# Graph attention, 1 core: TensorE's projection units are taken out of order, and a bank's second product follows its reader by a step

## The chip, the cores and the metric

The kernel runs on one core of a Trainium2 chip. Its engines are TensorE (PE in the profile), VectorE (DVE), ScalarE (ACT), GpSimd (POOL) and SyncE (SP), which issues transfers. The metric is the device time of one run in microseconds (us); lower is better.

## What is computed

The input x has 16 batches of 1024 nodes with 512 features, in float32; adj is one sparse 1024 x 1024 matrix of zeros and ones for all batches. Each batch goes through one layer of masked attention with 8 heads, a residual sum and a layer norm:

```python
q, k, v = x @ Wq + bq, x @ Wk + bk, x @ Wv + bv      # 8 heads of 64 features
scores = q @ k.T / sqrt(64), where adj is 0: -1e9
out = softmax(scores) @ v
result = layernorm(x + out @ Wo + bo)
```

## The kernel before

**Work and tiles.** A batch's 1024 nodes are 8 tiles of 128 rows. The rows of K and V are written to DRAM, and GpSimd gathers from there, for each tile of nodes, the rows that its nodes are linked to, one gather ("block") at a time. VectorE multiplies q with the gathered keys (`qk`) and reduces to scores (`s`), ScalarE takes the exponentials and weighs the values (`pv`), TensorE or VectorE adds the weighed values up (`sum`), VectorE normalises (`o`), TensorE transposes (`poT`) and multiplies with Wo (`po`), and VectorE and ScalarE make the residual sum and the layer norm (`y`, `stats`).

**The order of the work.** The program is written out under a manual schedule: the loop at the end of the main function runs over steps n, one for each block, and every engine runs its instructions in the order in which this loop issues them. In each step it issues the attention work of the blocks near n; then it spends a credit, in us of TensorE, on units from one of two lists: `finishing` (the products po of a finished tile) if there are any, otherwise `fronts` (all projections of all batches, in order). Transposes poT and the mean product pm come through a third list, `urgent`. Each unit is a tuple of its cost, a function that issues it, and a test whether it is ready. The loop looks only at the first unit of the list; if that isn't ready, the step ends. `later(k, fn)` puts the issue of fn k steps later. "Ready" is a matter of this writing order, not of time on the chip: an instruction that depends on another is safe in any case, and waits on a semaphore where its input isn't there yet.

**The projections of two tiles.** The function `pair` lists the units for x tiles 2j and 2j+1 of batch b. Keys and values of the two are made with seven half products in place of eight (Strassen's scheme in Winograd's form): on VectorE the sums s1 to s4 of the transposed tiles (`combine`, L783 to L786), and then on TensorE, each a unit of two matmuls into a 128 x 512 bank (L956):

1. bank x: A11·B11, read by ScalarE's copy e (L969)
2. bank p6: s2·T2, read by VectorE's w (L972)
3. q0: four matmuls of the query product pq of the first tile (L799)
4. bank x again: + A12·B21, which goes on top and needs the copy e first; read by ScalarE as the keys of the first tile (L835)
5. bank p7: s3·T3, read by VectorE's g (L975)
6. the transposes pxT of the next two x tiles (L757); ScalarE copies each to `xT` (L761), and a step after the second copy `combine` makes the next pair's s1 to s4
7. bank z: s1·T1, read by VectorE's kv (L984), which sets R["v1"]
8. q1: pq of the second tile (left out for tile 1 from batch 1 on, so in pair 0)
9. bank p4: A22·T4, read by VectorE's kv (L979)
10. bank z again: + s4·B22, which needs the read of L984 first; read by VectorE as the values of the first tile (L988)

After the tenth the second tile of K and V is sent to DRAM by SyncE, VectorE adds the values to `vsum` (L860 to L863), and after the last pair of a batch TensorE takes their mean, pm (L867). The products x, z and p write float32 with the two matmuls of a unit; the banks x and z exist once each, and four more banks ("fill") serve p6, p7, p4, pq, po, pxT, poT and pm in turn.

The unit's test before is `(need is None or need in R) and (b, j) in SX and bool(combined)`: the second product into x is ready as soon as e is in R, so in the very step in which the copy was issued, and that into z as soon as the read was issued. q products have no test.

Of the kernel before, what the change touches and what calls it, by code (L numbers as in the profile page):

```python
# [71 lines left out]
LAST_SHARE = 3.4  # L72
BIAS = 0.22

P = 128
# [103 lines left out]
def kernel(  # L179
# [62 lines left out]
    W = {}  # L242
# [12 lines left out]
    with ExitStack() as main:  # L255
# [6 lines left out]
        def fill_psum(name):  # L262
            return psum.tile([P, HALF], F32, tag="fill", name=name, bufs=4)
# [472 lines left out]

        BOTH = {}
        X, XT, SX, KV, VSUM, NRM, Y, OT, PS = {}, {}, {}, {}, {}, {}, {}, {}, {}
        set_up = {}
# [12 lines left out]
        def transpose_x(b, t):  # L752
            def pe():
# [25 lines left out]

                def combine():  # L780
                    s = [work.tile([P, HD2], F32, tag=f"s{i}", name=f"s{i}_{b}_{t}", bufs=1 + i // 4) for i in (1, 2, 3, 4)]
                    x0, x1 = XT[b, t - 1], XT[b, t]
                    nc.vector.tensor_tensor(s[0], x1[:, 0:HD2], x1[:, HD2:D], op=OP.add)  # L783
                    nc.vector.tensor_tensor(s[2], x0[:, 0:HD2], x1[:, 0:HD2], op=OP.subtract)
                    nc.vector.tensor_tensor(s[1], s[0], x0[:, 0:HD2], op=OP.subtract)
                    nc.vector.tensor_tensor(s[3], x0[:, HD2:D], s[1], op=OP.subtract)  # L786
                    SX[b, t // 2] = s
# [4 lines left out]

        def product(name, lhs, w, out):

            def unit(c):
                if c == 0:
                    PS[name] = fill_psum(name)
                p = PS[name]
                nc.tensor.matmul(p, lhs(c), w[:, c, :], start=(c == 0), stop=(c == NPAIR - 1))  # L799
                if c == NPAIR - 1:  # L800
                    del PS[name]
                    later(1, lambda: out(p))

            return [(PRODUCT, lambda c=c: unit(c), None) for c in range(NPAIR)]

# [10 lines left out]
        def pair(b, j):  # L816
# [62 lines left out]
            def lone_product():  # L879
# [24 lines left out]

                return [(4 * BIAS, pe, None)]

            def lhs(i):
                return lambda c: XT[b, tt[i]][:, ts(c, P)]

            q0, q1 = (  # L910
                product(f"pq_{b}_{tt[i]}", lhs(i), W["q"], lambda p, i=i: out_q(i, p)) if b == 0 or tt[i] != ONE_KEY else []
                for i in range(2)
            )
            if j == 0 and b >= PAIRED_FROM:
                q0 = []
                if merged(b):
                    q0 = product(f"pq_{b}_0", lambda c: BOTH[b // 2][:, 1, c, :], W["q"], lambda p: out_q(0, p))
                    q0 += lone_product()
# [28 lines left out]

            def unit(bank, left, right, first, after, need):
                def pe():
                    if first:  # L950
                        R[bank] = fill_psum(f"p{bank}_{b}_{j}") if bank[0] == "p" else psum.tile(
                            [P, HALF], F32, tag=bank, name=f"{bank}_{b}_{j}", bufs=1
                        )
                    l = left()
                    for c in range(2):
                        nc.tensor.matmul(  # L956
                            R[bank], l[:, ts(c, P)], right[:, c, :], start=(first and c == 0), stop=(c == 1),
                            skip_group_check=True,
                        )
                    later(1, after)  # L960

                return [(2 * PRODUCT, pe, lambda: (need is None or need in R) and (b, j) in SX and bool(combined))]

# [4 lines left out]
            def out_e():  # L968
                nc.scalar.copy(temp("e"), R["x"])  # L969

            def out_w():
# [5 lines left out]
            def out_k1():  # L977
                kv = KV[b, tt[1]]
                nc.vector.tensor_tensor(kv[:, 0:D], R["p4"], R["g"], op=OP.add)  # L979
                send(1)  # L980
                later_last(1, lambda: norm(b, tt[1], kv[:, 0:D]))

            def out_v1():
                nc.vector.tensor_tensor(new_kv(1)[:, D:], R["z"], R["g"], op=OP.add)  # L984
                R["v1"] = True

            def out_v0():
                nc.vector.tensor_tensor(KV[b, tt[0]][:, D:], R["z"], R["w"], op=OP.add)  # L988
                send(0)

            def s(i):
# [5 lines left out]
            units += q0  # L997
            units += unit("x", lambda: a(0, 1), B21, False, lambda: out_k(0, R["x"]), "e")
            units += unit("p7", s(3), T3, True, out_g, None)
# [499 lines left out]
        def paced(share, n):  # L1499
# [3 lines left out]
            return share * load_of(n) * (start[b + 1] - start[b]) / sum(load_of(m) for m in range(start[b], start[b + 1]))  # L1503

        prep = {}
        for t, n in REST_FROM.items():
# [9 lines left out]
        with tc.manual_schedule():  # L1516
# [21 lines left out]
            while n < total or plan or rest or urgent or done or finishing or spilled or lone_tiles or not guarded:  # L1538
# [53 lines left out]
                while credit > 0 or urgent:  # L1592
# [10 lines left out]
                    if not units:  # L1603
# [3 lines left out]
                        break  # L1607
                    cost, fn, ready = units[0]
                    if ready and not ready():
                        if urgent:  # L1610
                            urgent.pop(0)()
                            continue
                        break
                    del units[0]
                    fn()
# [42 lines left out]
```

## Time and profile before

| | us |
|---|---|
| time, median of 3 runs | 1847.21 |
| fastest and slowest run | 1845.62, 1847.80 |
| the profiled execution: span from the first to the last instruction | 1840.4 |
| the profiled execution's own time outside its span | not recorded |
| TensorE busy | 1798.2 |
| VectorE busy | 1693.7 |
| ScalarE busy | 1563.2 |
| GpSimd busy | 1215.3 |
| mean granted TensorE clock | 0.996 |

The profile is of one execution. A row of the timeline gives the start, the duration, the engine, the line, the operation with its output and inputs, the shapes, and how many such instructions follow each other (x4). Matmuls are pipelined, so a row's duration overlaps with the next row; what a product takes is read from start to start. One 128 x 512 float32 product leaves two records of a matmul, so a unit of two is a row "x4". Where an engine idled before a row, the row ends with that idle time and with what it waited for. Line numbers of the profile before are those of the code above; in the changed kernel they stand some lines lower (L956 is L971, L799 is L805, L757 is L759, L761 is L763, L984 is L1005, L867 is L873).

### The profile page before, as it was taken

To read this page: it belongs to the slowest core of one execution; us is meant where nothing else is said; L and a number is where in the kernel's file an instruction comes from. 1 tells how busy PE (TensorE), PEld (TensorE's weight loads), DVE (VectorE), ACT (ScalarE), POOL (GpSimd) and SP (SyncE) were. 2 spreads that over 40 slices of the span, in tenths; PEclk is the share of its full clock that TensorE was granted. 3 is DMA by queue.
4 is the path that set the end of the run, shared out by engine and by line. 5 is a ranking of instruction groups with operands and counts; after the bars stand their busy time and mean duration, and the time that the engine had idled before them with its cause. 6 is when DMAs were issued, how large, how long until landed. Compare 5 with 4: busy or idle time off the path is not lost.

```text
span 1840.4 us, 25352 instructions
## 1 busy us (share of the span) xinstructions
PE 1798.2 (98%) x5140; PEld 876.2 (48%) x5140; DVE 1693.7 (92%) x3473; ACT 1563.2 (85%) x6183; POOL 1215.3 (66%) x1142
## 2 busy tenths in 40 slices
PE   7999999999999999999999999999999999999997
PEld 3444454554444454444444445444544444444443
DVE  6889889999989999999999999999999999997986
ACT  3637869989889898999889988989799999987886
POOL 1367766766565776767757666677666767665786
PEclk9999999999999999999999999999999999999998
DMA  7358787989889899999988998999989999889995
GB/s 287 106 190 253 256 325 237 346 301 327 308 280 314 295 336 319 344 316 308 347 316 310 346 335 276 343 321 322 339 315 325 314 355 326 306 324 325 338 319 191
DMA packets 198791, 558.54 MB, mean 303 GB/s; under 512 B 33450, under 2 KB 33470, under 8 KB 198626
## 3 DMA queue, kind: packets, MB, share of 16 engines
q0 software_dynamic: 112640, 370.50, 59.3%
q1 hardware_dynamic: 82910, 180.52, 26.2%
q10 hardware_dynamic: 3076, 5.82, 0.9%
q14 instruction: 122, 1.00, 0.2%
q8 instruction: 43, 0.70, 0.2%
HBM read 420.30 MB, written 157.45 MB: 314 GB/s over the span
## 4 chain that ended last, share of the span: by engine, by line
PE 69%; DVE 10%; ACT 9%; DMA 4%; issue 3%; POOL 1%; SPq 0%; POOLq 0%; DVEq 0%; ACTq 0%
PE po L799 17%; PE pq L799 15%; PE pp L956 12%; PE z L956 9%; PE x L956 9%; ACT pv L1341 5%; DVE qk L1313 2%; PE poT L1401 2%; PE pxT L757 2%; PE sum L1367 2%; DVE s L1317 2%; PE sum L1366 2%; DVE pv L1357 1%; ACT sq_k L809 1%; DMA kvg<-kv_pair,place_row 1%
## 5 line engine op out<-in xcount | busy, mean ns | idle before, releaser
L1341 ACT ACTIVATE pv<-kvg,pv 128x64 f32<-128x64 f32 x3600 | 907.5, 341 | 0.0
L1292 POOL DMA_INDIRECT kvg<-kv_pair,place_row x462 | 526.7, 1140 | 307.4 <-ACT pv L1341 99.6
L799 PE MATMUL pq<-wq,xT 128*128 128x512 f32 x792 | 367.8, 596 | 0.0
L1317 DVE TENSOR_REDUCE s<-qk 128x8 f32<-128x512 f32 x530 | 360.7, 681 | 6.8
L799 PE MATMUL po<-wo,oT 128*128 128x512 f32 x792 | 359.3, 594 | 0.7 <-ACT oT L1405 0.7
L1313 DVE TENSOR_TENSOR qk<-qt,kvg 128x512 f32<-128x512 f32 x434 | 297.2, 685 | 1.1 <-DMA kvg<-kv_rows,key_row 0.6
L956 PE MATMUL x<-b,xT 128*128 128x512 f32 x504 | 237.3, 593 | 0.5 <-ACT e L969 0.4
L956 PE MATMUL pp<-t,s 128*128 128x512 f32 x504 | 237.0, 593 | 0.0
L1357 DVE TENSOR_TENSOR pv<-pv,pv 128x520 f32<-128x520 f32 x329 | 228.3, 694 | 4.3 <-ACT pv L1341 4.2
L799 PEld LDWEIGHTS po<-wo,oT 128*128 128x128 f32 x792 | 149.1, 191 | 170.0 <-issue 160.2
L799 PEld LDWEIGHTS pq<-wq,xT 128*128 128x128 f32 x792 | 148.4, 192 | 161.9 <-issue 149.9
L1010 POOL DMA_INDIRECT x<-in_x_dram,asked_row x120 | 133.0, 1108 | 77.8 <-issue 21.3
L1148 POOL DMA_INDIRECT out_dram<-y,asked_row x129 | 146.9, 1139 | 39.1 <-issue 21.2
L1328 ACT ACTIVATE pv<-s,absent 128x8 f32<-128x8 f32 x434 | 127.0, 294 | 44.0 <-DVE s L1317 40.8
L809 ACT ACTIVATE sq_k<-kv 128x128 bf16<-128x128 f32 x512 | 150.8, 301 | 6.4 <-DVE kv L979 3.4
L956 PEld LDWEIGHTS pp<-t,s 128*128 128x128 f32 x504 | 94.7, 191 | 108.1 <-issue 99.4
L956 PEld LDWEIGHTS x<-b,xT 128*128 128x128 f32 x504 | 94.2, 191 | 107.4 <-issue 99.0
L956 PE MATMUL z<-b,s 128*128 128x512 f32 x252 | 119.2, 596 | 7.0 <-DVE kv L984 7.0
L1246 POOL DMA_INDIRECT qg<-q_rows,query_row x96 | 104.4, 1088 | 28.4 <-issue 26.9
L956 PE MATMUL z<-t,s 128*128 128x512 f32 x252 | 118.6, 593 | 0.0
L956 PE MATMUL pp<-t,xT 128*128 128x512 f32 x252 | 118.5, 593 | 0.0
L1134 ACT ACTIVATE y<-y,stats 128x512 f32<-128x512 f32 (+1 forms) x128 | 102.7, 806 | 17.0 <-DVE stats L1129 17.0
(279 smaller groups left out, 2713.0 us busy)
## 6 DMA issues: line engine op xcount, KB each, us to landing
kv_pair<-kv SPq DMA_DIRECT2D x98, 512.0 KB
q_rows<-q SPq DMA_DIRECT2D x106, 256.0 KB
qt<-q_rows SPq DMA_DIRECT2D x98, 256.0 KB
residual<-x SPq DMA_DIRECT2D x83, 256.0 KB
y<-residual SPq DMA_DIRECT2D x83, 256.0 KB
kv_rows<-kv SPq DMA_DIRECT2D x15, 512.0 KB
kvg<-kv_pair,place_row POOLq DMA_INDIRECT x462, 6.9
kv_pair<-kv SPq DMA_DIRECT2D x28, 256.0 KB
```

Source lines behind the costliest of these rows:

```text
L799: nc.tensor.matmul(p, lhs(c), w[:, c, :], start=(c == 0), stop=(c == NPAIR - 1))
L809: nc.scalar.activation(sq, s[:, ts(h, P)], AF.Square, scale=scale, accum_out=sums[:, h:h + 1])
L956: nc.tensor.matmul(R[bank], l[:, ts(c, P)], right[:, c, :], start=(first and c == 0), stop=(c == 1), skip_group_check=True,)
L1010: nc.gpsimd.indirect_dma_start(out=y, out_offset=None, in_=x_rows, in_offset=bass.IndirectOffsetOnAxis(ap=asked_row[:, t:t + 1], axis=0), ...
L1148: nc.gpsimd.indirect_dma_start(out=out_rows[b, t], out_offset=bass.IndirectOffsetOnAxis(ap=rows, axis=0), in_=y, in_offset=None, element_o ...
L1246: nc.gpsimd.indirect_dma_start(out=q, out_offset=None, in_=q_rows[b % ROWS], in_offset=bass.IndirectOffsetOnAxis(ap=rows, axis=0))
L1292: nc.gpsimd.indirect_dma_start(out=KG[n], out_offset=None, in_=rows, in_offset=bass.IndirectOffsetOnAxis(ap=(place_row if b else key_row)[ ...
L1313: nc.vector.tensor_tensor(QK[n], q, KG[n][:, 0:D], op=OP.mult)
L1317: nc.vector.tensor_reduce(S[n], QK.pop(n).rearrange("p (h d) -> p h d", d=HD), axis=AX.X, op=OP.add)
L1328: nc.scalar.activation(PV[n][:, D:], S.pop(n), AF.Exp, bias=bias)
L1341: nc.scalar.activation(pv[:, ts(h, HD)], v[:, ds(D + h * HD, HD)], AF.Copy, scale=pv[:, D + h:D + h + 1])
L1357: nc.vector.tensor_tensor(PV[b, t], PV[b, t], pv, op=OP.add)
```

## The change

(1) The second product into bank x or z is ready only when its reader was issued in an earlier step: R["copied"] and R["v1"] hold the step, and the test compares it with the current one. (2) A count `busy` keeps a later pair from starting a bank, and from overwriting s1 to s3, before the readers of the earlier one are issued (`combine` then tries again a step later), and p7 stays behind p6, p4 and z behind p7. (3) The loop no longer looks at the first unit only: `next_unit` takes the first ready one of the next ten, and stops its search at a transpose that isn't first in the list. The query products get a test of their own, that the transposed tile exists, which it does from the step in which its copy was issued.

```diff
@@ -71,6 +71,7 @@
 START_SHARE = 2.0
 LAST_SHARE = 3.4
 BIAS = 0.22
+LOOK = 10
 
 P = 128
 
@@ -735,6 +736,7 @@
 
 
         BOTH = {}
+        busy = {"x": 0, "z": 0, "p6": 0, "p7": 0, "s": 0}
         X, XT, SX, KV, VSUM, NRM, Y, OT, PS = {}, {}, {}, {}, {}, {}, {}, {}, {}
         set_up = {}
 
@@ -778,6 +780,10 @@
                         later(1, combine)
 
                 def combine():
+                    if busy["s"]:
+                        later(1, combine)
+                        return
+                    busy["s"] = 3
                     s = [work.tile([P, HD2], F32, tag=f"s{i}", name=f"s{i}_{b}_{t}", bufs=1 + i // 4) for i in (1, 2, 3, 4)]
                     x0, x1 = XT[b, t - 1], XT[b, t]
                     nc.vector.tensor_tensor(s[0], x1[:, 0:HD2], x1[:, HD2:D], op=OP.add)
@@ -790,7 +796,7 @@
 
             return [(TRANSPOSE, pe, lambda: (b, t) in X)]
 
-        def product(name, lhs, w, out):
+        def product(name, lhs, w, out, ready=None):
 
             def unit(c):
                 if c == 0:
@@ -801,7 +807,7 @@
                     del PS[name]
                     later(1, lambda: out(p))
 
-            return [(PRODUCT, lambda c=c: unit(c), None) for c in range(NPAIR)]
+            return [(PRODUCT, lambda c=c: unit(c), ready) for c in range(NPAIR)]
 
         def squares(name, s, sums, scale=1.0):
             for h in range(NPAIR):
@@ -902,19 +908,19 @@
                     later_last(1, out)
                     later(3, lambda: nc.vector.tensor_reduce(lone_hat[:, b // 2:b // 2 + 1], norms, axis=AX.X, op=OP.max))
 
-                return [(4 * BIAS, pe, None)]
+                return [(4 * BIAS, pe, lambda: (b, 0) in XT)]
 
             def lhs(i):
                 return lambda c: XT[b, tt[i]][:, ts(c, P)]
 
             q0, q1 = (
-                product(f"pq_{b}_{tt[i]}", lhs(i), W["q"], lambda p, i=i: out_q(i, p)) if b == 0 or tt[i] != ONE_KEY else []
+                product(f"pq_{b}_{tt[i]}", lhs(i), W["q"], lambda p, i=i: out_q(i, p), lambda i=i: (b, tt[i]) in XT) if b == 0 or tt[i] != ONE_KEY else []
                 for i in range(2)
             )
             if j == 0 and b >= PAIRED_FROM:
                 q0 = []
                 if merged(b):
-                    q0 = product(f"pq_{b}_0", lambda c: BOTH[b // 2][:, 1, c, :], W["q"], lambda p: out_q(0, p))
+                    q0 = product(f"pq_{b}_0", lambda c: BOTH[b // 2][:, 1, c, :], W["q"], lambda p: out_q(0, p), lambda: (b, 0) in XT)
                     q0 += lone_product()
             n = b * NT + 2 * j + 2
             xt = [u for t in (n, n + 1) if t < B * NT for u in transpose_x(t // NT, t % NT)]
@@ -946,12 +952,21 @@
                 return XT[b, tt[i]][:, ts(h, HD2)]
 
             def unit(bank, left, right, first, after, need):
+                def ready():
+                    if (b, j) not in SX or not combined or need is not None and R.get(need, now[0]) >= now[0]:
+                        return False
+                    behind = {"p7": "p6", "p4": "p7", "z": "p7"}.get(bank)
+                    return not first or not busy.get(bank) and (behind is None or behind in R)
+
                 def pe():
                     if first:
+                        busy[bank] = 2 if bank == "p7" else bank != "p4"
                         R[bank] = fill_psum(f"p{bank}_{b}_{j}") if bank[0] == "p" else psum.tile(
                             [P, HALF], F32, tag=bank, name=f"{bank}_{b}_{j}", bufs=1
                         )
                     l = left()
+                    if any(l is t for t in SX[b, j][:3]):
+                        busy["s"] -= 1
                     for c in range(2):
                         nc.tensor.matmul(
                             R[bank], l[:, ts(c, P)], right[:, c, :], start=(first and c == 0), stop=(c == 1),
@@ -959,7 +974,7 @@
                         )
                     later(1, after)
 
-                return [(2 * PRODUCT, pe, lambda: (need is None or need in R) and (b, j) in SX and bool(combined))]
+                return [(2 * PRODUCT, pe, ready)]
 
             def temp(name):
                 R[name] = work.tile([P, D], F32, tag=name, name=f"{name}_{b}_{j}", bufs=1)
@@ -967,6 +982,11 @@
 
             def out_e():
                 nc.scalar.copy(temp("e"), R["x"])
+                R["copied"] = now[0]
+
+            def out_k0():
+                out_k(0, R["x"])
+                busy["x"] = 0
 
             def out_w():
                 nc.vector.tensor_tensor(temp("w"), R["p6"], R["e"], op=OP.add)
@@ -977,16 +997,19 @@
             def out_k1():
                 kv = KV[b, tt[1]]
                 nc.vector.tensor_tensor(kv[:, 0:D], R["p4"], R["g"], op=OP.add)
+                busy["p7"] -= 1
                 send(1)
                 later_last(1, lambda: norm(b, tt[1], kv[:, 0:D]))
 
             def out_v1():
                 nc.vector.tensor_tensor(new_kv(1)[:, D:], R["z"], R["g"], op=OP.add)
-                R["v1"] = True
+                R["v1"] = now[0]
+                busy["p7"] -= 1
 
             def out_v0():
                 nc.vector.tensor_tensor(KV[b, tt[0]][:, D:], R["z"], R["w"], op=OP.add)
                 send(0)
+                busy["z"] = busy["p6"] = 0
 
             def s(i):
                 return lambda: SX[b, j][i - 1]
@@ -995,7 +1018,7 @@
             units += unit("x", lambda: a(0, 0), B11, True, out_e, None)
             units += unit("p6", s(2), T2, True, out_w, None)
             units += q0
-            units += unit("x", lambda: a(0, 1), B21, False, lambda: out_k(0, R["x"]), "e")
+            units += unit("x", lambda: a(0, 1), B21, False, out_k0, "copied")
             units += unit("p7", s(3), T3, True, out_g, None)
             units += xt
             units += unit("z", s(1), T1, True, out_v1, None)
@@ -1501,6 +1524,15 @@
                 return share
             b = blocks[n][0]
             return share * load_of(n) * (start[b + 1] - start[b]) / sum(load_of(m) for m in range(start[b], start[b + 1]))
+
+        def next_unit(units):
+
+            for i, (cost, _, ready) in enumerate(units[:LOOK]):
+                if cost == TRANSPOSE and i:
+                    return None
+                if not ready or ready():
+                    return i
+            return None
 
         prep = {}
         for t, n in REST_FROM.items():
@@ -1605,13 +1637,13 @@
                             urgent.pop(0)()
                             continue
                         break
-                    cost, fn, ready = units[0]
-                    if ready and not ready():
+                    at = next_unit(units)
+                    if at is None:
                         if urgent:
                             urgent.pop(0)()
                             continue
                         break
-                    del units[0]
+                    cost, fn, _ = units.pop(at)
                     fn()
                     credit -= cost
                     first_unit = False
```

TensorE runs the same products. Its order differs at some places, mostly in pair 0 of a batch, and comes together again a few products later in most of them. Three of these follow. In the rows, z_9_0 is bank z of batch 9, pair 0; x_9_1 the x bank of its pair 1; xT_9_2 transposed tile 2 of batch 9; a row of a unit is x2 (two matmuls).

TensorE, batch 9, pair 0, where the second z product stands; before:

```order
L956 MATMUL z_9_0_10666<-t1_102,s1_9_1_10395 128x512 x2
L956 MATMUL pp4_9_0_10701<-t4_105,xT_9_1_10359 128x512 x2
L956 MATMUL z_9_0_10666<-b22_101,s4_9_1_10398 128x512 x2
L956 MATMUL x_9_1_10736<-b11_99,xT_9_2_10685 128x512 x2
L1401 MATMUL poT_7_5_10739<-ident_58,o_7_5_10681 128x128 x4
```

And in the changed kernel:

```order
L971 MATMUL z_9_0_10666<-t1_102,s1_9_1_10395 128x512 x2
L971 MATMUL pp4_9_0_10701<-t4_105,xT_9_1_10359 128x512 x2
L805 MATMUL pq_9_2_10704<-wq_63,xT_9_2_10685 128x512
L971 MATMUL z_9_0_10666<-b22_101,s4_9_1_10398 128x512 x2
L1424 MATMUL poT_7_5_10737<-ident_58,o_7_5_10681 128x128 x4
L971 MATMUL x_9_1_10742<-b11_99,xT_9_2_10685 128x512 x2
```

The first of four matmuls of pq on the new tile 2 stands ahead of the second z product now, and x of the next pair has gone behind a transpose poT.

TensorE, batch 10, pair 0; before:

```order
L956 MATMUL z_10_0_11883<-t1_102,s1_10_1_11620 128x512 x2
L956 MATMUL pp4_10_0_11886<-t4_105,xT_10_1_11583 128x512 x2
L956 MATMUL z_10_0_11883<-b22_101,s4_10_1_11623 128x512 x2
L956 MATMUL x_10_1_11925<-b11_99,xT_10_2_11875 128x512 x2
L1366 MATMUL sum_8_7_11321<-pv_287_11816,sums_106 128x256
L1367 MATMUL sum_8_7_11321<-pv_287_11816,sums_106 128x264
L956 MATMUL pp6_10_1_11966<-t2_103,s2_10_3_11904 128x512 x2
```

And in the changed kernel:

```order
L971 MATMUL z_10_0_11883<-t1_102,s1_10_1_11620 128x512 x2
L971 MATMUL pp4_10_0_11886<-t4_105,xT_10_1_11583 128x512 x2
L971 MATMUL x_10_1_11923<-b11_99,xT_10_2_11866 128x512 x2
L805 MATMUL pq_10_2_11926<-wq_63,xT_10_2_11866 128x512 x2
L1389 MATMUL sum_8_7_11321<-pv_287_11816,sums_106 128x256
L1390 MATMUL sum_8_7_11321<-pv_287_11816,sums_106 128x264
L971 MATMUL z_10_0_11883<-b22_101,s4_10_1_11623 128x512 x2
```

Here x of the next pair, half of its pq and the sum of an attention tile have moved ahead of the second z product, which stood right behind p4.

TensorE, batch 15, pair 3, the last of the projections (po_14_3 is the output product of tile 3 of batch 14, pm_15 the mean over vsum); before:

```order
L956 MATMUL pp4_15_3_18966<-t4_105,xT_15_7_18718 128x512 x2
L956 MATMUL z_15_3_18927<-b22_101,s4_15_7_18764 128x512 x2
L799 MATMUL po_14_3_19019<-wo_64,oT_14_3_18532 128x512 x4
L1366 MATMUL sum_14_7_18375<-pv_485_18900,sums_106 128x256
L1367 MATMUL sum_14_7_18375<-pv_485_18900,sums_106 128x264
L867 MATMUL pm_15_19079<-vsum_15_18174,mean_86 1x512
```

And in the changed kernel:

```order
L971 MATMUL pp4_15_3_18968<-t4_105,xT_15_7_18719 128x512 x2
L805 MATMUL po_14_3_18995<-wo_64,oT_14_3_18539 128x512 x4
L971 MATMUL z_15_3_18929<-b22_101,s4_15_7_18766 128x512 x2
L1389 MATMUL sum_14_7_18376<-pv_485_18900,sums_106 128x256
L1390 MATMUL sum_14_7_18376<-pv_485_18900,sums_106 128x264
L873 MATMUL pm_15_19097<-vsum_15_18276,mean_86 1x512
```

The output product has moved from behind the second z product to ahead of it; between z and pm only the sum is left.

On VectorE the sums s1 to s4 of a next pair stand behind other steps where `combine` is held back: in batch 5, pair 0, they stood ahead of y of tile 2 of batch 3, a product qk_122 and its reduction, and stand behind these now, right ahead of the read of z.

## The prediction

> **What bounds the kernel now.** I read the page first, then the waits of TensorE, then the timeline at each wait. From the page, the span, the busy time of the engines and the chain that ended last:
>
> ```profile
> span 1840.4 us, 25352 instructions
> PE 1798.2 (98%) x5140; PEld 876.2 (48%) x5140; DVE 1693.7 (92%) x3473; ACT 1563.2 (85%) x6183; POOL 1215.3 (66%) x1142
> PE 69%; DVE 10%; ACT 9%; DMA 4%; issue 3%; POOL 1%; SPq 0%; POOLq 0%; DVEq 0%; ACTq 0%
> ```
>
> TensorE is busy 98% of the span and holds 69% of the chain. The change leaves its products as they are and only reorders them, so it can win no more than TensorE's idle time, 1840.4 − 1798.2 = 42.2 us at most. The waits of TensorE (what it waited for: us in total, times, longest) show how little of that a change of order reaches:
>
> ```profile
> PE z L956 <- DVE kv L984: 7.0, 5, 3.0
> PE poT L1401 <- DVE stats L1123: 3.1, 1, 3.1
> ```
>
> The first row is the target: the second product into bank z waits until VectorE has read the first one out of it. There are 63 such pairs of x tiles (four in each of 16 batches, less the first), and only 5 waited, 7.0 us together. That is 0.4% of the span, and 3.7 us (0.2%) is about what a measurement of this kernel can tell from no change.
>
> **Gains: second products that now stand behind a ready one.** I count from start to start: a unit of two half products (x4 rows) takes 1.72 us when another follows at once, so what exceeds that is stall. Timeline of pair 0 of batch 10, then of 5, and pair 1 of batch 1 (start, us, engine, line, tile, wait):
>
> ```profile
> 1060.99 1.88 PE L956 MATMUL pp<-t,xT 128*128 128x512 f32 x4
> 1062.05 0.58 ACT L761 COPY xT<-pxT 128x512 f32<-128x512 f32 x1
> 1065.14 0.68 DVE L984 TENSOR_TENSOR kv<-z,g 128x512 f32<-128x512 f32 x1
> 1065.88 1.98 PE L956 MATMUL z<-b,s 128*128 128x512 f32 x4 [3.01 <-DVE kv L984]
> 1067.70 1.88 PE L956 MATMUL x<-b,xT 128*128 128x512 f32 x4
> ...
> 544.95 0.43 DVE L783 TENSOR_TENSOR s<-xT 128x256 f32<-128x256 f32 x1 [2.96 <-PE z L956]
> 546.39 0.59 PE L1366 MATMUL sum<-pv,sums 128*128 128x256 f32 x2
> 549.08 0.68 DVE L984 TENSOR_TENSOR kv<-z,g 128x512 f32<-128x512 f32 x1
> 549.82 1.98 PE L956 MATMUL z<-b,s 128*128 128x512 f32 x4 [2.38 <-DVE kv L984]
> ...
> 141.98 1.88 PE L956 MATMUL pp<-t,xT 128*128 128x512 f32 x4
> 144.92 1.98 PE L956 MATMUL z<-b,s 128*128 128x512 f32 x4 [1.06 <-DVE kv L984]
> ```
>
> At batch 10 the second z now follows the next pair's x, a q product and a sum. The x needs the copy of the next tile, done at 1062.05 + 0.58 = 1062.63, before TensorE is free at 1060.99 + 1.72 = 1062.71. The stall of 1065.88 − 1062.71 = 3.17 goes whole: x and two of the four products of q fill 3.4 us, until after 1065.82, when VectorE's read ends. At 5 only x comes between (547.27 to 548.99; the two sums from 546.39 take 0.88). VectorE must read z by 548.99. In before it idles 2.96 us on the first z product, because the sums s1 to s4 of the next pair overwrite a buffer that this product reads; in after these four stand behind two steps of y, a product and a reduction, so they fill that idle, and the read ends near 548. Gain 549.82 − 547.27 = 2.55. At 1: 144.92 − 143.70 = 1.22. The wait at batch 7 is what the row of 7.0 leaves beside 3.01, 2.38, 1.06 and the 0.39 of batch 14 below: 0.16. Together 7.10.
>
> **Losses: q products that now stand ahead and wait for a copy.** Readiness is decided when the order is written: a tile counts as there once its copy from PSUM was issued, in the same step. Rule (1) asks a step of distance of the z and x banks, but not of the q products, whose new test only asks whether the tile exists. So where x of the next pair is not ready (it needs the sums s1 to s4, issued a step after the copies), the first q product on the next tile goes ahead of z, and TensorE waits for ScalarE's copy instead. Timeline of pair 0 of batches 8, 9 and 14:
>
> ```profile
> 853.37 1.88 PE L956 MATMUL pp<-t,xT 128*128 128x512 f32 x4
> 855.22 1.98 PE L956 MATMUL z<-b,s 128*128 128x512 f32 x4
> 855.52 1.03 ACT L761 COPY xT<-pxT 128x512 f32<-128x512 f32 x2
> ...
> 960.63 1.88 PE L956 MATMUL pp<-t,xT 128*128 128x512 f32 x4
> 962.34 1.88 PE L956 MATMUL z<-b,s 128*128 128x512 f32 x4
> 963.68 1.07 ACT L761 COPY xT<-pxT 128x512 f32<-128x512 f32 x2
> 964.33 1.13 PE L956 MATMUL x<-b,xT 128*128 128x512 f32 x2
> ...
> 1479.55 0.60 PE L1401 MATMUL poT<-ident,v 128*128 128x128 f32 x4
> 1480.54 1.98 PE L956 MATMUL z<-b,s 128*128 128x512 f32 x4 [0.39 <-DVE kv L984]
> 1480.80 1.03 ACT L761 COPY xT<-pxT 128x512 f32<-128x512 f32 x2
> ```
>
> The rows hold two copies, the first of which takes 0.58 (batch 10's row); with some 0.05 for the semaphore the tile is usable 0.63 after the row's start. At 8: 856.13, while TensorE is free at 853.37 + 1.72 = 855.09: it waits 1.04, where z waited 0.13, so +0.91. At 9: usable at 964.32 against 962.35, a wait of 1.97; before, z ran there, and x behind it then lost 964.33 − 964.06 = 0.27; so +1.70. At 14: 1481.43 against 1479.55 + 0.43 = 1479.98, a wait of 1.45 in place of 0.56; +0.89. Together +3.50. Behind the waiting q product stand z, poT and x on TensorE. VectorE's second read of z and the send of the tile come that much later; the gathers that need the batch are some ten blocks away. ScalarE's copy is not pulled forward by the wait, since TensorE hands it nothing new.
>
> **One more loss, at batch 15.** There the output product po of tile 3 of batch 14 now stands ahead of the second z, instead of behind it. What follows is VectorE's vsum and then the mean pm, which TensorE reaches when it comes:
>
> ```profile
> 1671.67 1.88 PE L956 MATMUL z<-b,s 128*128 128x512 f32 x4
> 1673.39 3.60 PE L799 MATMUL po<-wo,oT 128*128 128x512 f32 x8
> 1673.59 0.69 DVE L988 TENSOR_TENSOR kv<-z,w 128x512 f32<-128x512 f32 x1 [1.02 <-PE z L956]
> 1676.12 1.41 DVE L863 TENSOR_TENSOR vsum<-vsum,kv 128x512 f32<-128x512 f32 x2
> 1677.79 1.02 PE L867 MATMUL pm<-vsum,mean 128*1 128x512 f32 x2
> ```
>
> From z's end at 1673.39 to vsum's end at 1676.12 + 1.41 = 1677.53 pass 4.1 us, 4.2 with a semaphore. In before po (3.44) and a sum (0.88) lie in that stretch, 4.32, and pm waits 0.1. In after po lies ahead of z and only the sum is left: a new wait of 4.2 − 0.88 = 3.3, net +3.2. Bounds: VectorE may do the four steps between kv and vsum earlier, as z is later against it; the three vector steps themselves (0.69 + 1.41) leave a wait of 1.2, net +1.1. I take +3.2, since the steps between come from the same stream.
>
> **Edits that cost nothing.** The swaps of x and p7 at the head of a pair (batches 0, 2, 4, 6, 10, 12), and the held-back sums s1 to s4, move products within margins of 0.1 to 3.1 us in which the trace has no wait; if that cover goes, each costs the 0.1 to 0.6 of a copy. One output tile becomes a plain one, with one more VectorE step (about 0.6), off TensorE's path.
>
> **The end.** From batch 15 on, TensorE runs one output product (four rows, 3.4 us) later against the other engines:
>
> ```profile
> 1808.33 1.02 PE L1401 MATMUL poT<-ident,o 128*128 128x128 f32 x4 [3.09 <-DVE stats L1123]
> 1809.14 3.25 PE L799 MATMUL po<-wo,oTs 128*128 128x512 f32 x4
> 1812.44 1.88 PE L799 MATMUL po<-wo,oTs 128*128 128x512 f32 x4
> 1826.54 3.70 PE L799 MATMUL po<-wo,oT 128*128 128x512 f32 x8 [0.49 <-ACT oT L1405]
> ```
>
> The last wait, 0.49 and 0.16 around it, goes, since more work lies ahead of it: −0.65. The 3.09 at 1808.33 I keep: the transpose there waits for VectorE, which itself is paced by TensorE's po products before.
>
> The unit of products after that wait took 3.25 instead of 1.88, so an idle stretch of 3.1 us there cost another 1.4; after the 3.01 at 1065.88 the next unit took 1.88, so it cost nothing. The Trainium skill (TensorE: Matmul & The Clock Gate, Part 1: The HAM clock gate) says that the clock halves after an idle window of 3.4 us whose phase runs free. By that rule the two rows differ by phase, and the new 3.3 us at pm may fall either way; no run here shows the phase.
>
> **Sum.** −7.10 + 3.50 + 3.2 − 0.65 = −1.05 on the span: 1839.35. The profiled execution has only its span; the median run, 1847.21, is 6.8 longer, and the runs differ by 2.2, so I carry 6.8 for what lies around: 1846.2.
>
> **Rivals.** *A, faster: VectorE gets ahead at the end.* If VectorE no longer follows the po products there, the transpose at 1808.33 finds its input ready: 3.09, 0.16 around it and the 1.4 of slow products go, 1846.2 − 4.65 = 1841.5. For it: TensorE is one product behind from 1680 on. Against: VectorE's own waits between 1676 and 1805.
>
> ```profile
> DVE y L1113 <- PE po L799: 8.4, 10, 1.5
> ```
>
> Ten waits for po: it is paced by TensorE. Chance 0.20.
>
> *B, slower: the lag stays at the end.* The output product that moved to the end of TensorE's order lies behind the last transpose of batch 15, whose time VectorE sets. If VectorE has no idle left to give, its stream ends where it did, and one po product, 3.4 to 3.65, is appended, and if of the 3.60 won net at z (7.10 − 3.50) nothing is passed on either, as much again: 1849.8 to 1853.4. It decides when the 8.4 above does not shrink. Against: each of the ten waits can absorb some. Chance 0.20.
>
> *C, the clock.* The 3.3 us at pm halve the clock as at 1808: +1.4, 1847.6. Chance 0.12. The same page (HAM oscillation) sets about 3.4 us of idle as the limit; the row at 1808.33 shows the price already at 3.1, and the measurement decides.
>
> *D, it doesn't do what it says.* Where x is not ready, as at batches 0, 6, 11 and 13, z still follows p4 directly, and if the q copies cost as much as z did, nothing is left: 1847.2. Chance 0.08.
>
> **Numbers.** The forecast has 0.40. Faster by over 0.2% (under 1843.5): A, 0.2, and 0.04 from the forecast's spread. Slower by over 0.2% (over 1850.9): B's upper part, 0.16, and 0.05 from the forecast, if several covers fail. The rest, 0.55, is within 0.2%. The range runs from A's 1841.5, less 1.0, to near B's upper end: 1840.5 to 1853.
>
> **What would show it.** Right: no wait of z for kv at batches 1, 5, 7 and 10; waits of 1.0, 2.0 and 1.5 of a q product for the copy xT at 8, 9 and 14; pm waiting some 3 us for vsum at 1677. Wrong: q waits at further batches (the test of existence is then the whole story); pm without a wait; a last po that starts more than 3 us later than 1826.5 (B), or a poT at 1808 without a wait (A).

## The result, and the profile after

| | before | changed |
|---|---|---|
| median of 7 runs each, us | 1846.42 (1844.56 to 1849.67) | 1851.41 (1850.22 to 1855.79) |
| ratio to before, 95% interval | | 1.0023 (1.0013 to 1.0034) |
| span of the profiled execution, us | 1840.4 | 1848.4 |

The changed kernel is slower by 0.23%. The time lies in the forecast range, on the side that was given 0.21; the likeliest case, no change, was wrong. Beside the kernel before in two later jobs the changed kernel measured 1.0028 (1.0018 to 1.0037) and 0.9994 (0.9976 to 1.0011). In one later run (e8) two of twelve executions took 3889 and 6052 us, which nothing here explains; the ratios leave them out.

From the page of the changed kernel, the span, the busy time and the chain; and then TensorE's waits:

```profile
span 1848.4 us, 25355 instructions
PE 1797.9 (97%) x5140; PEld 875.3 (47%) x5140; DVE 1693.4 (92%) x3473; ACT 1563.8 (85%) x6183; POOL 1233.8 (67%) x1142
PE 84%; DVE 8%; issue 2%; ACT 2%; DMA 2%; POOL 1%; SPq 0%; POOLq 0%; DVEq 0%; ACTq 0%
```

```profile
PE poT L1424 <- DVE o L1410: 12.2, 4, 9.0
PE pm L873 <- DVE vsum L869: 6.3, 4, 3.2
PE pq L805 <- ACT xT L763: 4.0, 3, 1.8
```

TensorE does the same work; z is no longer in the list of waits. The three waits of q products and the longer wait of pm are there as forecast. What was not forecast is the first row: one transpose waits 9.0 us. The places, in the timeline of the changed kernel (batches 5 and 10, then 8, 9 and 14, then pm of batch 15):

```profile
548.21 1.88 PE L971 MATMUL x<-b,xT 128*128 128x512 f32 x4
549.93 1.88 PE L971 MATMUL z<-b,s 128*128 128x512 f32 x4
...
1062.46 1.88 PE L971 MATMUL x<-b,xT 128*128 128x512 f32 x4
1064.17 1.88 PE L805 MATMUL pq<-wq,xT 128*128 128x512 f32 x4
...
853.99 1.12 PE L805 MATMUL pq<-wq,xT 128*128 128x512 f32 x2 [0.88 <-ACT xT L763]
...
963.11 1.12 PE L805 MATMUL pq<-wq,xT 128*128 128x512 f32 x2 [1.83 <-ACT xT L763]
...
1477.60 1.12 PE L805 MATMUL pq<-wq,xT 128*128 128x512 f32 x2 [1.27 <-ACT xT L763]
...
1672.23 1.88 PE L971 MATMUL z<-b,s 128*128 128x512 f32 x4
1678.16 1.02 PE L873 MATMUL pm<-vsum,mean 128*1 128x512 f32 x2 [3.18 <-DVE vsum L869]
```

And the end: TensorE's last transpose but one, with the unit behind it; VectorE's waits for GpSimd ahead of it; and GpSimd's own:

```profile
1811.28 1.12 PE L1424 MATMUL poT<-ident,o 128*128 128x128 f32 x4 [9.02 <-DVE o L1410]
1812.19 3.62 PE L805 MATMUL po<-wo,oTs 128*128 128x512 f32 x4
...
1792.89 0.23 DVE L1152 SCALAR_TENSOR_TENSOR stats<-stats 128x1 f32<-128x1 f32 x2 [3.01 <-POOL stats L1197]
1796.08 0.16 DVE L1152 SCALAR_TENSOR_TENSOR stats<-stats 112x1 f32<-112x1 f32 x1 [2.96 <-POOL stats L1149]
...
1784.69 0.95 POOL L1061 DMA_INDIRECT y<-in_x_dram,asked_row  x1 [2.90 <-DMA out_dram<-y,asked_row]
```

Read from the bottom: GpSimd waits 2.90 us for a store, because the next load takes the store's buffer; VectorE waits twice 3 us for steps queued on GpSimd behind it; so `o` of the last tile but one comes 3 us later than before, and TensorE, which reaches its transpose 3.0 us earlier than before (1802.3 against 1805.2), waits 9.0 in place of 3.1. TensorE is earlier there because one output product has moved behind this transpose: 48 matmul records of po with wo follow it, against 40 before, and from the transpose's start to the end it takes 37.2 us, against 32.1.

**By stages.** I cut each trace at two instructions that all kernels have: the first transpose pxT of batch 5, and the first z product of the last pair.

| trace | from pxT of batch 5 to z of the last pair | from there to the end |
|---|---|---|
| before; run r1 | 1161.1; 1164.9 | 176.0; 178.4 |
| changed; r2; r5 | 1157.3; 1159.0; 1157.2 | 186.9; 187.7; 189.9 |
| e1; r3 (last pair as before) | 1158.2; 1160.2 | 177.8; 177.8 |
| e7 (slip kept, end as before) | 1158.2 | 177.4 |
| e8; r7 (before, end late) | 1161.7; 1162.6 | 185.2; 183.8 |

The middle got some 4 to 5 us shorter; the last 180 us got about 10 us longer; the medians show the difference, 5.0 us. The runs r1, e1 and so on are described below.

### The profile page after: what moved, and what is told of

It reads as the page before. It is cut to its first block, busy times and chain, and to the rows that moved or that the text cites. A ratio compares the mean times of both kernels' runs of the same rounds, so it can differ in the third digit from the quotient of the medians.

```text
span 1848.4 us, 25355 instructions
## 1 busy us (share of the span) xinstructions
PE 1797.9 (97%) x5140; PEld 875.3 (47%) x5140; DVE 1693.4 (92%) x3473; ACT 1563.8 (85%) x6183; POOL 1233.8 (67%) x1142
## 4 chain that ended last, share of the span: by engine, by line
PE 84%; DVE 8%; issue 2%; ACT 2%; DMA 2%; POOL 1%; SPq 0%; POOLq 0%; DVEq 0%; ACTq 0%
PE po L805 18%; PE pq L805 18%; PE pp L971 15%; PE x L971 10%; PE z L971 10%; PE pxT L759 3%; PE poT L1424 3%; PE sum L1390 2%; PE sum L1389 2%; DVE qk L1336 2%; DVE s L1340 1%; ACT pv L1364 1%; DVE pv L1380 1%; PE pm L873 1%; DMA b<-in_L_gnn_Wk_dram 1%
## 5 line engine op out<-in xcount | busy, mean ns | idle before, releaser
L1315 POOL DMA_INDIRECT kvg<-kv_pair,place_row x462 | 532.4, 1152 | 292.8 <-ACT pv L1364 81.9
L1269 POOL DMA_INDIRECT qg<-q_rows,query_row x96 | 108.9, 1134 | 28.2 <-issue 27.0
```

Of the source, the lines that this page charges most:

```text
L1269: nc.gpsimd.indirect_dma_start(out=q, out_offset=None, in_=q_rows[b % ROWS], in_offset=bass.IndirectOffsetOnAxis(ap=rows, axis=0))
L1315: nc.gpsimd.indirect_dma_start(out=KG[n], out_offset=None, in_=rows, in_offset=bass.IndirectOffsetOnAxis(ap=(place_row if b else key_row)[ ...
```

## The experiments

**What is late, and why.** In the program's own order the second z product of the last pair slips from step 483 to 484, since rule (1) keeps it a step behind its reader. It is the last unit in `fronts`. In step 484 the list is therefore not empty, and the kernel before's tests of that (L1544, L1582, L1588, L1598) keep the share of the step at 1.87 us instead of 3.4, load the residual rows of one finished tile instead of two, and start no reload of a spilled tile. (A fifth test, L1557, also holds back three gathers for that one step; e7 leaves it as it is, and its end is back all the same.) From there to the end each finished tile's product stands a step later against VectorE's blocks. That gave theory 1: the loss is this slip. Theory 2: the loss is in the middle, in the waits for xT. Theory 3: the loss is the wait of pm.

The runs came in four jobs. In the first (r1, e1, e7, e8) and the last (e12, r5 to r7) the kernel before had medians of 1845.49 and 1845.29 us; the chips of the second (e9, e3, e5, e10) and third (r2 to r4, e11) varied more, with medians of 1866.56 and 1871.62 and 17 to 24 us between its fastest and slowest run, and there the ratios tell less. Their traces show where most of the extra time lies: the stretch ahead of the first pxT of batch 5 takes 512 to 527 us in them and 502 to 505 in all others; so the two later stages can be compared across jobs better than the whole times.

**r1: the kernel before against itself.** 

> The kernel before, unchanged, timed against itself: ratio 1.000 within the interval under every theory. What it adds is a second profile of it. If the first profile (span 1840.4 us) was a typical one, this span is within 1 us of it; if it was a short one, this span is near its time less 1.9 us (what lies around the span in all seven runs of the changed kernel), so near 1844.5 us.

Measured 0.9998 (0.9986 to 1.0009); its profiled execution took 1848.74 us with a span of 1846.9, and in every run shown with its span 1.8 to 1.9 us lie around it. So the profile of before that the prediction rests on was one of the shortest executions of this kernel (35 runs here: 1842.26 to 1852.66), and the 8.0 us between the two spans overstate the change. Timeline of r1 at batch 10, and a stretch of its windows (length, busy time by engine, then the granted clock):

```profile
1066.72 2.75 PE L956 MATMUL z<-b,s 128*128 128x512 f32 x4 [3.00 <-DVE kv L984]
1069.27 2.85 PE L956 MATMUL x<-b,xT 128*128 128x512 f32 x4
```

```profile
1067.80:1071.20 3.40, 3.40 (x6) 1.34 (x5) 2.44 (x5) 0.00 (x0) 2.79 (x3) 0.50 0.91 304
```

The same wait of 3.0 us as in the first profile is followed here by 3.4 us at half clock, which cost 1.7. The waits that the change removes carry such a price in some executions (r7 and e12 show it behind the wait of z at batch 5). Of the 3.8 us by which r1's middle stage is longer than that of the first profile, 3.4 are clock: two such windows, where the first profile has none.

**e1: the slip undone.**

```diff
-  need is not None and R.get(need, now[0]) >= now[0]
+  need is not None and R.get(need, now[0] + 1) >= now[0] + ((b, j) == (B - 1, NT // 2 - 1))
```

> The changed kernel, but in the last pair of the last batch the second z product is ready in the step of its reader again, so it is issued a step earlier, as in the kernel before. Theory 1 (the loss is at the end: that last unit slips a step, and with it everything that waits for the list of projections to be empty): all other places keep their gains and losses, which the two traces put at -2.8 us up to pm, so 2.8 us faster than the kernel before (ratio 0.9985), and no wait of pm for vsum over 0.5 us. Theory 2 (the loss is in the middle, in the q products that wait for copies and what they delay; the end absorbs a step): still 3 to 5 us slower than before (ratio 1.002 or more).

Measured 0.997 (0.9959 to 0.9982), 1840.15 us; again as r3 beside the changed kernel:

> The kernel of run e1 again (the changed kernel, but the last pair's second z product in the step of its reader), now beside the changed kernel: 0.997 of before, and 9 to 10 us under the changed kernel, if the loss of the change is all at that one unit.

> The changed kernel, unchanged, on the chip of the three runs below: 1.0023 of before, as measured at first, if its loss does not depend on the chip; the reference for those three.

Measured 0.9944 (0.9921 to 0.9967) for r3 and 0.9994 (0.9976 to 1.0011) for r2. Both times one unit's step is worth 0.5%. In e1's timeline pm comes without a wait and the transpose at the end waits about as in before:

```profile
1673.60 1.02 PE L873 MATMUL pm<-vsum,mean 128*1 128x512 f32 x2
...
1804.91 0.66 PE L1424 MATMUL poT<-ident,o 128*128 128x128 f32 x4 [3.54 <-DVE stats L1146]
```

The q waits for xT are all still there in e1 (4.0 us), so theory 2 falls.

**e7: the slip kept, its effect on the finished tiles taken away.**

```diff
-  ... / max(fronts_end - n, 1) + NS * SUM / NBT if fronts else LAST_SHARE
+  ... / max(fronts_end - n, 1) + NS * SUM / NBT if len(fronts) > 1 else LAST_SHARE
-  for tile_done in done[:0 if fronts and len(done) < LAZY else 1 if fronts else 2] + coming:
+  for tile_done in done[:0 if fronts and len(done) < LAZY else 1 if len(fronts) > 1 else 2] + coming:
-  if spilled and not fronts and n > last_reload + 1 ...
+  if spilled and len(fronts) < 2 and n > last_reload + 1 ...
```

> The changed kernel, with the last unit still a step late (so pm still waits about 3.3 us for vsum), but the three tests of the last phase (the share of a step, the load of residual rows, the reload of spilled tiles) count the list of projections as empty when one unit is left, so that the finished tiles go on in the steps of the kernel before. Theory 1: the end is as in before, the wait of pm stays: -2.8 + 3.3 = +0.5 us against before (ratio 1.0003, same). Theory 2, and a theory 3 (the wait of pm itself, with what it does to the clock, is the loss): 4 us slower than before, as the changed kernel.

Measured 0.9976 (0.9965 to 0.9988), 1841.22 us. So the end is back without undoing the slip. But the wait of pm did not stay, which I had not seen: the second finished tile has its residual rows in time, and its product now fills the stretch ahead of pm.

```profile
1676.27 3.60 PE L805 MATMUL po<-wo,oT 128*128 128x512 f32 x8
1679.80 1.02 PE L873 MATMUL pm<-vsum,mean 128*1 128x512 f32 x2
```

e7 thus cannot tell theory 1 from 3. The next one can.

**e8: the late end alone, in the kernel before.**

```diff
   credit += paced(share, n) if n >= 0 else share
+  credit -= 1.77 * (n == total - 46)
```

> The kernel before, with 1.77 us less credit for TensorE in the one step after the last projection, and nothing else: the order up to there is that of before, and from there the finished tiles' products stand one step later, with the list of finished tiles in the last 20 steps as in the changed kernel. Theory 1: slower by what the end costs, 4 to 7 us (ratio 1.002 to 1.004), with TensorE waiting 6 us or more for the last but one transpose poT instead of 3.1. Theories 2 and 3: the end absorbs it, within 1 us of before.

Measured 1.0039 (1.0029 to 1.0049), 1853.43 us. In the last job it ran again as r7:

> The kernel of e8 again, as the reference for the run above: 1.0039 of before.

Measured 1.0036 (1.0023 to 1.0049). In e8 z waits as in before, pm waits at most 1.0 us, and the transpose at the end:

```profile
1812.88 1.11 PE L1401 MATMUL poT<-ident,o 128*128 128x128 f32 x4 [10.30 <-DVE stats L1123]
1813.80 3.62 PE L799 MATMUL po<-wo,oTs 128*128 128x512 f32 x4
```

A late end alone costs 7 us; theory 1 is shown, and theory 3 can hold no more than the rest, about 3 of the 10. One thing differs: in e8's written order the reloads of spilled tiles fall a step behind only from step 498 on, in the changed kernel from step 484, so e8 is not the changed kernel's late end in every step.

**e10 and e12: how much of it is GpSimd's wait.** The load in question, y_15_8, stands nine rows earlier on GpSimd in the changed kernel, right behind the store of y_15_1, since the loop asks how many residual rows it holds, and in the late end it holds fewer at that step. The store that it waits for, whose buffer it takes, is that of y_15_2, three rows ahead of it. e10 is the changed kernel, e12 that of e8, each with

```diff
-  if lone_tiles and kept_y() < 4:
+  if lone_tiles and kept_y() < 4 and (fronts or n >= total - 12):
```

> The changed kernel, with its late end, and one load moved: the gather of residual rows for the last shared tile (y_15_8 on GpSimd), which there comes right behind the store whose buffer it takes and waits 2.9 us for it, is held until the step in which before has it. If GpSimd's wait is what makes VectorE wait twice 3 us for its power steps, and so TensorE 9 us for the last but one transpose, then VectorE's two waits shrink to 2.2 or less, TensorE's wait to about 6, and the time by 3 us (ratio to before about 1.0007 instead of 1.0023). If the end is late only because one more output product is left behind the transpose, nothing changes: ratio 1.0023.

Measured 0.9988 (0.9962 to 1.0014) on one of the varying chips, which settles nothing. So it was run again as r6, beside the changed kernel as r5 and beside e12 and e8.

> The kernel of e10 again (the changed kernel with the gather of y_15_8 held), beside the changed kernel: 3 us under it if GpSimd's wait is worth that in the changed kernel too, equal to it if not.

> The changed kernel, as the reference for the run above: between 0.9994 and 1.0023 of before, the two values measured.

> The kernel of e8 (the kernel before with the late end alone), with the gather of y_15_8 held to the step in which before has it, as in e10. If GpSimd's wait for the store makes about 3.4 us of the late end, as the traces of e10 and of the changed kernel say, this is 3 to 4 us under e8 in one job, 1.002 of before where e8 is 1.0039. If the trace of e10 misled, it equals e8.

Measured in that job: changed 1.0028 (1.0018 to 1.0037), 1850.15 us; e10 1.0005 (0.9992 to 1.0018), 1847.07; e8 1.0036; e12 1.0029 (1.0017 to 1.0042). The waits of the changed kernel (r5: GpSimd's, then VectorE's) and of e10 (r6: VectorE's, and the transpose) in it:

```profile
POOL y L1061 <- DMA out_dram<-y,asked_row: 4.6, 1, 4.6
DVE stats L1152 <- POOL stats L1197: 4.3, 1, 4.3
DVE stats L1152 <- POOL stats L1149: 3.0, 1, 3.0
```

```profile
DVE stats L1152 <- POOL stats L1149: 2.9, 2, 2.2
...
1809.36 0.69 PE L1424 MATMUL poT<-ident,o 128*128 128x128 f32 x4 [4.84 <-DVE stats L1146]
```

So in the changed kernel GpSimd's wait is worth some 3 us of the loss, as expected. The output product that has moved behind the transpose stays there: in r6 36.1 us follow the transpose's start, against 32.1 in before and in r1. No run takes that part away by itself.

In e8's kernel (r7 in this job) the same step brought 0.6 us between medians of 7 and 5 runs, where 3 to 4 were expected; the two intervals overlap. The stage from z of the last pair to the end is 181.8 in e12 against 183.8 to 185.2. In e12's trace GpSimd's wait for the store is gone there and TensorE's wait for the transpose is 4.9 instead of 10.2 and 10.3; but this execution lost time elsewhere, at a reload whose order is the same in both kernels, where r7 waited 0.4 and e8 1.5, with 3.4 us at half clock behind it:

```profile
PE poT L1401 <- DVE stats L1123: 4.9, 1, 4.9
PE po L799 <- DMA oTs<-spill: 2.9, 1, 2.9
```

So the trace of e12 shows the step at work, and why the medians show so little of it stays open.

**e3 and e5: which half of the change gains.** e3 sets LOOK = 1 (and keeps e1's line); e5 has the look ahead with `need not in R` as the whole test.

> The changed kernel, with the last pair as in e1, and without the look ahead: only the first unit of the list is tried, so a second z or x product that is not ready ends the step, and what gets ahead of it is only the sums, transposes and finished products of the next step. If the look ahead brings the gain in the middle, the wait at batch 10 shrinks only by a sum (3.0 to about 2.1) and the whole is 1 to 3 us faster than before (ratio 0.9985 to 0.9995). If the step of distance alone brings it, all z waits go and no q product waits for a copy: 7 us faster or more (ratio 0.996).

> The changed kernel with the look ahead, but second products ready in the step of their reader again, everywhere. Nearly all places then have the order of before, since a second z product is always ready when its turn comes: z keeps its five waits of 7 us, time as before (ratio 0.9995 to 1.0005). If the look ahead by itself moves time, it differs by more than 1 us.

e3: 1.0001 (0.9977 to 1.0026); e5: 0.9985 (0.9957 to 1.0013). The times only bound it; the traces are clear. z still waits in both in the middle, 2.9 us in e3 and 3.7 in e5, and their middle stage is 1161.6 and 1162.0 us, as long as in the kernel before. At batch 10 in e3:

```profile
1089.52 3.38 PE L971 MATMUL z<-b,s 128*128 128x512 f32 x4 [2.12 <-DVE kv L1005]
```

Only a sum came ahead of z there. So it takes both: the rule makes z step back, the look ahead has something to put in its place.

**e9: q products a step behind the copy too.**

```diff
-  lambda i=i: (b, tt[i]) in XT
+  lambda i=i: AT.get((b, tt[i]), now[0]) < now[0]      # AT holds the step in which the copy was issued
```

> The changed kernel, with the last pair as in the run e1 (its second z product a step earlier, as in before), and with the q products ready only in the step after the copy of their tile, by the rule that the change gives the z and x banks. If the three waits of q products for the copy xT (4.0 us idle, 3.5 net of what stood there before) are paid on TensorE, they go and nothing takes their place: 3.5 us faster than e1, 9 us faster than before (ratio 0.995). If ScalarE and VectorE were the bound there, the q wait only moves to the next product: as e1, ratio 0.997.

Measured 0.9938 (0.9914 to 0.9962). Beside e1's kernel, in the job of r3:

> The kernel of run e9 again (as the one above, and the q products a step behind the copy of their tile), beside it: if the three waits for the copy xT cost TensorE their 4.0 us idle, less what stood at these places before, it is 2 to 4 us under the one above, 0.995 of before; if something else paces those places, equal to it.

Measured 0.995 (0.9925 to 0.9976), where e1's kernel had 0.9944. No gain over e1 that can be seen. The q waits are gone from its trace, but the q product had filled a stretch in which a mean now waits:

```profile
852.10 1.02 PE L874 MATMUL pm<-vsum,mean 128*1 128x512 f32 x2 [1.73 <-DVE vsum L870]
```

With small waits back at z and po as well, the middle stage is 1157.4 and 1158.4 against 1158.2 and 1160.2 in e1's kernel: 1 to 2 us of the 3.5.

**e11: a lead at the end.** e9 with `fronts_end = start[B - 1] - 14` instead of 12, the finished tiles two steps ahead of before.

> The kernel of e9, with the last projections spread over two steps less, so that the list of projections is empty two steps earlier and the finished and reloaded tiles go through two steps ahead of the kernel before. If the end is paced by how early TensorE gets through the finished tiles, it gains: up to the 3.1 us of the wait for the last but one transpose and the 1.7 us of the slow window behind it, so 2 to 5 us under e9. If at the end of before VectorE and its blocks pace the end and only a lag hurts, a lead brings nothing, or loses 1 to 3 us, since TensorE then waits longer for the same transpose.

0.9953 (0.9934 to 0.9971): nothing gained over e9 (0.995 in the same job) that these runs can show, and its stage from z of the last pair to the end is 183.6, against 180.8 and 177.9 in e9's kernel. A lag costs; a lead brought nothing. e1's kernel already beats the kernel before and the changed one, by 0.3% in the first job and 0.56% in the third against before, and neither e9 nor e11 is faster than it by more than the noise.

## Why the prediction was wrong

- **Gains at z: right.** Forecast 3.17, 2.55, 1.22 and 0.16. All five waits are gone; x starts at 1062.46, when p4 ends, and z at 549.93 follows x at once.
- **Losses at q: right.** Forecast from start to start 1.04, 1.97 and 1.45; the changed trace shows 853.99 − 852.95 = 1.04, 963.11 − 961.12 = 1.99 and 1477.60 − 1476.17 = 1.43.
- **pm: right.** Forecast 3.3, measured 3.18.
- **The middle as a whole: right in sign, too small.** From batch 5 on my terms give −2.4; the two first traces give 1157.3 − 1161.1 = −3.8. The rest are further stalls under 0.6 us each at po, x, z and pxT that went too. And the price of half clock behind a z wait was missing: by r1 it is 1.7 us, in some executions.
- **The end: the step that failed.** I wrote "The 3.09 at 1808.33 I keep: the transpose there waits for VectorE, which itself is paced by TensorE's po products before", and booked a gain of 0.65 at the last wait. The wait became 9.02, and from pm's start to the end the changed kernel takes 170.3 us (171.0 and 173.3 in r2 and r5) where before takes 162.6 (165.0 in r1). TensorE was indeed one product later against the others, and I saw it, but I took that for a shift without a price. Two things were not worked out: that VectorE's stream at the end passes through GpSimd's queue, whose loads take buffers that late tiles free late (some 3 us, by r5 and r6), and that the product that stood ahead of the transpose as cover is missing there and is still to be done behind it.
- **Rival B had the sign and, by its price of 3.65 to 7.25, the time** (1849.8 to 1853.4; measured 1851.41), and the sign that the prediction named for it came: the last po starts at 1833.31, 6.8 us later than in before. Its other test, that VectorE's wait for po does not shrink, decides nothing: it is 8.4 in the first profile of before, and in the same stretch of the changed kernel and of r1, the kernel before again,

```profile
DVE y L1136 <- PE po L805: 10.6, 12, 1.8
DVE y L1113 <- PE po L799: 11.7, 14, 1.6
```

  Its mechanism was half right: one output product does lie behind the transpose now, but VectorE's stream does not end where it did. Its products qk stood 1.5 to 5 us ahead of the first profile of before up to 1742 us, within 1.7 us of it from there to 1789, and 3.0 to 4.3 us after it behind the two waits for GpSimd.
- **Why the lag arises at all, I did not ask.** The order showed one output product moved; that it came from a list that is not empty for one step more, and that the tests of the last phase hang on that, could be read in the loop. That is where 0.20 for B was too little.
- **Rival C: not in this profile, true in the others.** Granted clock (the third figure from the end) in the stretch from 1677.40 to 1680.80, in the changed kernel, where pm starts at 1678.16, and then in r5, where it starts at 1676.13:

```profile
1677.40:1680.80 3.40, 2.64 (x6) 0.98 (x7) 3.40 (x6) 2.42 (x10) 0.00 (x0) 1.00 1.04 381
```

```profile
1677.40:1680.80 3.40, 3.40 (x5) 1.33 (x4) 2.95 (x7) 2.88 (x11) 0.00 (x0) 0.51 1.03 408
```

  The wait of pm was 3.18 and 3.17 in the two. The other traces with this wait (r2, e10, r6) have half clock behind it as well, so the 0.12 was too little for it.
- **The 6.8 us around the span was wrong:** it is 1.9, and the profiled execution was a short one. The absolute forecast took no harm, as the sum was a difference put on the median.

## What to carry to other kernels

Where a schedule changes phase when a list becomes empty, a rule that delays the last entry by one step delays the whole last phase: look at what tests the list, and price one step of lag there by itself (here 7 us by itself, and about 10 with the wait of pm, against 4 to 5 us won over all the rest). A wait on an engine is not removed by moving another product into it if that product waits for something else; ask of everything that goes ahead what its own input is, and of everything that is left behind what it used to cover. And take more than one profile of the kernel before when the matter is 0.2%.

## What the runs showed of the hardware

TensorE's granted clock goes in windows of 3.4 us with a fixed phase in each execution. I summed TensorE's idle time in every window of the 18 traces, without the first 60 us and the last 10 us of each: of 100 windows at full clock that were idle for 1.0 to 1.92 us, none was followed by a window at half clock; of 51 that were idle for 2.03 us or more, all were; between them, 5 of 12. So a wait of 3 us costs nothing when the edge of a window cuts it near its middle (pm in the first trace of the changed kernel, 1.5 and 1.7 us) and 1.7 us more when one window holds over 2 us of it (z in r1, 0.7 and 2.3 us), and the waits of q, 1.83 at most, never cost clock here. The Trainium skill (TensorE: Matmul & The Clock Gate, Part 1: The HAM clock gate) states the window and its free phase, and these traces agree; it asks for a whole idle window, and here about 2.0 of 3.4 us were enough. At the end of the changed kernel 10.2 us run at half clock, the first 5.1 of them still within the wait of 9.0 us; e8 has 13.7 us in the same place:

```profile
1806.20:1816.40 10.20, 5.12 (x10) 2.75 (x11) 8.85 (x23) 10.20 (x38) 5.06 (x5) 0.50 0.37 139
```
